# A 64-image convolution, spectral-mixing and FFN kernel: the last 64 expanded channels computed unshifted, and shifted by transfers

## The chip, the cores and the metric

The kernel runs on one core of a Trainium2 chip, in one launch. The metric is device time in microseconds; the number given is the median of several runs. Beside these runs there is one execution under the hardware profiler, and every duration of a single instruction in this document comes from such an execution.

## What is computed

The input is 64 images of 96 channels by 56 x 56 pixels, all in fp32. Each image goes through two layers.

```
# layer 0: inverted residual block with a shift and a channel shuffle
out = silu(bn(einsum('bchw,oc->bohw', x, expand_w)))      # 96 -> 192 channels
out = shift(out)      # quarter 0 one row down, 1 one column right, 2 one row up, 3 one column left
out = channel_shuffle(out, groups=4)
out = silu(bn(bn(depthwise3x3(out)) + bn(out * id_w)))
out = out * sigmoid(grouped(relu(grouped(mean(out)))))    # squeeze and excitation
x   = silu(bn(einsum('bchw,oc->bohw', out, proj_w)) + x)  # 192 -> 96

# layer 1, on the 3136 tokens of an image
t = t + attn(layernorm(t))   # 96 -> 192, relu, FFT over tokens, per-channel complex
                             # scale and relu, inverse FFT, 192 -> 96
t = t + ffn(layernorm(t))    # 96 -> 384 -> 96 with inputs rounded to fp8
```

The shift moves every quarter of the 192 channels by one pixel, with zeros coming in at the edge. It follows the silu of the expansion, so a shifted value is the same number at another place.

## The kernel before, in words

**One image after another, many in flight.** Each image is cut into about sixty kinds of step (x_in, ea_mm, eb_mm, lt, f2_mm and so on), most with several numbered pieces: `ea_mm[3]` is strip 3 of `ea_mm`. The table `PLAN` gives each piece a time relative to its image's start, the image number times `PERIOD` is added, and the pieces of all 64 images are issued in the order of the sum. These times set nothing but an order. Every engine (TensorE = PE, VectorE = DVE, ScalarE = ACT, GpSimd = POOL) and the transfer queue of SyncE (SP) then works strictly in that order, and waits where an operand is not ready. All transfers of the loop are issued by SP. Pieces of up to four images stand between one another: while one image is expanded, the one before is in its convolution, and older ones are in the spectral layer and the FFN.

**Expansion.** The image lies in one buffer `x` (`xi` in the code) with a border of one pixel, on 112 partitions: 96 channels, one partition of ones that brings the bias, and a gap. The 192 expanded channels are kept in two tensors. `e_a` holds the first 32 channels of each of the four quarters, 128 channels, one per partition. `e_b` holds the other 16 channels of each quarter, 64 channels, and to fill the partitions the image is split into two row halves: partitions 0 to 63 hold the upper 28 rows, 64 to 127 the lower 28, each with one row of the other half and the border, which the 3 x 3 convolution needs.

`ea_mm` (L413) computes strips of 8 rows. It shifts by reading: for each quarter a matmul with 32 weight columns reads a window of `x` that is moved by one pixel (`window`), so what lands in PSUM is already shifted. `ea_ev` (L418) applies silu on ACT.

`eb_mm` (L430) does the same for `e_b`. A quarter is 16 channels here, [...] so two quarters with different windows share one block: a table `ex_b` of weights padded with zeros lets the first matmul (e = 0) write one quarter and zeros, and the second (e = 1) add the other. A piece of 7 rows takes eight matmuls: two values of `e`, two row halves `h`, two blocks `u`. There are four such pieces, and a fifth of one row that gives the row which each half needs of the other. `eb_ev` (L443, L445, L446) evicts them with silu into `e_b`.

**Convolution.** The depthwise convolution is divided among engines. For `e_a`, `dw_mm` (L475) does 36 of the 56 rows on PE with diagonal weights; it uses all four buffers of the PSUM pool `psb`. `gt` (L494, L496) does the other 20 rows on DVE in nine taps into `d_vec`. For `e_b`, `lt` (L507, L509) does all rows on DVE in nine taps into `d_last`; `lt[0]` is the middle tap, and it needs all of `e_b`. ACT then applies silu and sums (`dw_ev` L484, `gs` L499, `ls` L512).

**The rest, as far as it is spoken of here.** `se1`, `se2` compute the gate; `pj_mm` (L575 to L586), `pj_add` (L594) and `pj_ev` (L600) project, add `x` and write the tokens `t`. `x_in` (L198) loads the next image into `x` once `pj_add` has read it. `c_mm` (L626), `c_st` (L634), `c_v`, `c_pow`, `sp_v` (L658), `sp_mm`, `sp_ev`, `sp_ld` (L664) and `sp_st` (L683) compute the layernorm's statistics and put them where they are used. `w1_mm` (L696), `w1_ev` (L708), `f1_mm` (L723), `f1_ev` (L735), `f1_st` (L744) do the first matmul and the first part of the FFT and send the spectrum to DRAM; `f2_ld` (L753, L755) fetches it back in another order. The frequency stage is `f2_mm` (L769, L779), `f2_u` (ACT, L794), `f2_s` (DVE, L810, L813), `f2_r` (ACT, L817) and `f2_p` (DVE, L823), in six groups of which `f2_p[5]` is the last in the order. `w2_mm` (L834, L846) reads what `f2_p` wrote, `w2_ev` (L864) evicts, `i1_mm` (L873) and `i1_ev` (L885) begin the inverse, `i1_st` (L892) sends rows to DRAM, `i2_ld` (L897, L898) fetches them in two halves, a one-element `probe` between them waiting for the first half. `i2_mm` (L908) and `i2_ev` (L920) finish the inverse and add to `t`. The FFN is `n_mm` (L608), `n_sq` (L615), `n_v` (L619), `n_pow` (POOL, L936), `n_x` (L942), `x_mm` (L951), `x_ev` (L958), `h_mm` (L964), `h_ev` (L969), `h_b` (L974), `h_q` (L980), `o_mm` (L986), `o_ev` (L991), `o_b` (L996), `o_f` (POOL, L1002), and `o_st` (L1008), which stores the result. Matmul results of the spectral layer go to two large PSUM buffers, `psa`, used in turn; all others to the four of `psb`.

## Time and profile before

| what | value |
|---|---|
| three runs | 6729.68, 6730.21, 6732.37 us; median 6730.21 |
| the profiled execution | 6725.7 us, of which 6723.9 us is the span from the first to the last instruction |
| mean granted TensorE clock | 0.986 |
| busy in the span | PE 6152.3, DVE 5639.2, ACT 4384.5, POOL 1493.4 us |
| DMA | 689.44 MB, mean 103 GB/s |
| DVE waiting for `e_b` at `lt[0]` (L507) | 140.8 us in 64 waits |
| PE in the matmuls that write `ps_eb` (L430) | 367.0 us for 4096 records of 392 columns, 24.9 us for 1024 of 56 |

Two things help in reading. An fp32 matmul of the program is two records in the trace (4 matmuls of 392 columns, 2 values of `e`, 4 pieces, 64 images and two passes are the 4096 of the last row). And a line such as `3062.17 2.84 PE L430 MATMUL ps_eb<-x,ex_b ... x32` reads: from 3062.17 us after the span's start, for 2.84 us, 32 such records, named by what they write and read. In brackets stands how long the engine had been idle before, and what ended that wait.

### The profile page before, as it was taken

What the parts mean: (1) busy time and instruction counts of PE and PEld (TensorE: products, weight loads), DVE (VectorE), ACT (ScalarE), POOL (GpSimd) and SP (SyncE); (2) the same over time, 40 slices, a digit from 0 to 9 for tenths busy, and PEclk for the clock granted to TensorE, in tenths of its full rate; (3) what the DMA queues carried; (4) which work ended last, traced back from release to release, by engine and by line L of the source; (5) the groups of instructions that cost most, each with busy time, mean ns of one, the idle gap of its engine ahead of it and who ended that gap; (6) DMA issues with size and microseconds to landing.
All of it is one profiled execution on the core that took longest, in us unless ns stands there. A gap on an engine that the chain in (4) does not pass through costs nothing.

```text
span 6723.9 us, 246864 instructions
## 1 busy us (share of the span) xinstructions
PE 6152.3 (91%) x107010; PEld 4033.1 (60%) x107010; DVE 5639.2 (84%) x10903; ACT 4384.5 (65%) x8718; POOL 1493.4 (22%) x1035
## 2 busy tenths in 40 slices
PE   6999999999999999999999999999999999999996
PEld 3656655666656666566566666666665656656654
DVE  7888888888888888888888888888888888888884
ACT  2666666666666666666666666666666666666665
POOL 1212212222222222122222222221222222212212
PEclk9999999999999999999999999999999999999997
DMA  3344444344444444443444444444434444444333
GB/s 76 99 104 106 103 104 105 101 102 109 103 103 105 106 104 103 104 109 98 102 109 103 103 104 106 104 103 104 108 100 103 107 103 103 105 103 108 101 96 82
DMA packets 996378, 689.44 MB, mean 103 GB/s; under 512 B 671298, under 2 KB 944522, under 8 KB 995162
## 3 DMA queue, kind: packets, MB, share of 16 engines
q1 hardware_dynamic: 992570, 671.88, 39.1%
q8 instruction: 841, 13.78, 0.9%
q10 hardware_dynamic: 2720, 1.77, 0.1%
q14 instruction: 247, 2.02, 0.1%
HBM read 329.66 MB, written 341.31 MB: 100 GB/s over the span
## 4 chain that ended last, share of the span: by engine, by line
PE 43%; DVE 35%; ACT 12%; DMA 4%; issue 4%; POOL 1%; SPq 1%; POOLq 0%; ACTq 0%; DVEq 0%
PE ps_d L475 10%; DVE ue L813 6%; DVE buf_h L823 5%; DVE s L810 5%; PE psa L873 5%; ACT ue L794 4%; PE ps_ea L413 4%; PE psa L696 4%; PE ps_eb L430 4%; DVE buf_h L708 3%; DVE d_last L509 3%; PE psa L723 3%; DMA buf_h<-rows 3%; PE ps_c L626 3%; DVE y L974 3%
## 5 line engine op out<-in xcount | busy, mean ns | idle before, releaser
L1002 POOL TENSOR_TENSOR o<-t,o 112x448 f32<-112x448 f32 x448 | 688.7, 1537 | 3539.8 <-DVE o L996 1277.9
L509 DVE SCALAR_TENSOR_TENSOR d_last<-e_b,taps,d_last 128x1568 f32<-128x1568 f32 x512 | 1008.6, 1970 | 2.6
L980 ACT CAST h<-y 128x448 fp8e5<-128x448 f16 x1344 | 747.7, 565 | 167.9 <-DVE y L974 167.8
L496 DVE SCALAR_TENSOR_TENSOR d_vec<-e_a,taps,d_vec 128x1120 f32<-128x1120 f32 x512 | 766.1, 1496 | 13.9
L969 ACT CAST y<-ps_h 128x448 f16<-128x448 f32 x1344 | 692.0, 542 | 90.2 <-PE ps_h L964 79.9
L475 PE MATMUL ps_d<-e_a,diag 32*32 32x504 f32 x18432 | 710.6, 590 | 17.0 <-issue 16.9
L936 POOL TENSOR_TENSOR rs<-v,mhalf 112x4 f32<-112x4 f32 x448 | 450.0, 1012 | 1193.0 <-DVE v L620 1193.0
L696 PE MATMUL psa<-w1c,t 112*64 112x96 f32 x14336 | 652.5, 247 | 1.4 <-ACT fs L735 1.4
L696 PEld LDWEIGHTS psa<-w1c,t 112*64 112x64 f32 x14336 | 607.2, 137 | 73.7 <-DVE t L920 35.9
L794 ACT ACTIVATE ue<-psa,fa 128x448 f32<-128x448 f32 (+1 forms) x512 | 358.9, 704 | 381.3 <-DVE ue L813 355.8
L634 DVE BATCH_NORM_STATS2 st<-ps_c 112x6 f32<-112x96 f32 x1792 | 336.3, 249 | 313.4 <-PE ps_c L626 313.4
L475 PEld LDWEIGHTS ps_d<-e_a,diag 32*32 32x32 f32 x18432 | 392.0, 103 | 325.1 <-issue 69.8
L974 DVE TENSOR_SCALAR y<-y,qb 128x448 f16<-128x448 f16 x1344 | 510.2, 384 | 69.1 <-ACT y L969 65.2
L964 PE MATMUL ps_h<-xq,q 96*128 96x448 fp8e5 x1344 | 425.1, 359 | 131.2 <-ACT t L600 109.3
L769 PEld LDWEIGHTS psa<-l_tab,buf_g 128*64 128x64 f32 x7424 | 361.5, 137 | 241.1 <-issue 109.4
L615 ACT ACTIVATE sq<-ps_n 112x384 f32<-112x384 f32 x448 | 220.2, 492 | 430.6 <-PE ps_n L608 430.2
L769 PE MATMUL psa<-l_tab,buf_g 128*64 128x112 f32 x7424 | 414.6, 263 | 83.8 <-DVE ue L813 46.2
L834 PEld LDWEIGHTS psa<-w2a,buf_h 128*64 128x64 f32 (+1 forms) x7424 | 331.8, 135 | 218.8 <-issue 172.2
L653 POOL TENSOR_TENSOR rs<-v,mhalf 112x16 f32<-112x16 f32 (+1 forms) x128 | 338.0, 2640 | 494.0 <-DVE v L648 494.0
L723 PE MATMUL psa<-buf_h,f_tab 56*64 56x384 f32 x3584 | 401.6, 504 | 47.6 <-DVE buf_h L708 46.8
L810 DVE SCALAR_TENSOR_TENSOR s<-psa,fa,ue 128x448 f32<-128x448 f32 (+1 forms) x512 | 325.1, 635 | 137.3 <-ACT ue L794 137.2
L708 DVE SCALAR_TENSOR_TENSOR buf_h<-psa,rs_full 128x768 f32<-128x768 f32 (+1 forms) x512 | 424.8, 850 | 10.2 <-PE psa L696 9.0
(175 smaller groups left out, 12093.1 us busy)
## 6 DMA issues: line engine op xcount, KB each, us to landing
spec<-fs SPq DMA_DIRECT2D x896, 192.0 KB
buf_g<-spec SPq DMA_DIRECT2D x384, 336.0 KB
buf_h<-rows SPq DMA_DIRECT2D x128, 672.0 KB
x<-in_x SPq DMA_DIRECT2D x896, 84.0 KB
out_dram<-o SPq DMA_DIRECT2D x896, 84.0 KB
rows<-buf_g SPq DMA_DIRECT2D x128, 420.0 KB
rows<-buf_g SPq DMA_DIRECT2D x64, 504.0 KB
buf_g<-spec SPq DMA_DIRECT2D x128, 210.0 KB
```

Of the source, the lines that this page charges most:

```text
L475: nc.tensor.matmul(pss[r][j * 32 : j * 32 + 32], lhsT=diag[pr, tap, :], rhs=e_a[pr, r0 : r0 + SR, dx : dx + HW], start=tap == 0, stop=tap ...
L496: nc.vector.scalar_tensor_tensor(d_vec, win, w, d_vec, ALU.mult, ALU.add)
L509: nc.vector.scalar_tensor_tensor(d_last, win, w, d_last, ALU.mult, ALU.add)
L696: nc.tensor.matmul(ps[hc * 64 : hc * 64 + 64, k, 0:C], lhsT=t[:, n0 : n0 + 64], rhs=w1c[:, hc * C : hc * C + C], start=True, stop=True,)
L708: nc.vector.scalar_tensor_tensor(h_v[:, d * NJ + j0 : d * NJ + j0 + n, :], ps[:, 0:n, 0:C], 0.0, rs_full[:, d, j0 : j0 + n].unsqueeze(2).t ...
L769: nc.tensor.matmul(ps[c0 : c0 + 64, k, 0:CP], lhsT=g_v[:, k1, c0 : c0 + 64], rhs=l_tab[:, k1, :], start=True, stop=True,)
L794: nc.scalar.activation(held["ue", b, i][:, q, 0:n, :], held["f2", b, i][:, 0:n, 0:HW], AF.Identity, bias=par[:, 2 + q : 3 + q], scale=par[ ...
L810: nc.vector.scalar_tensor_tensor(held["s", b, i][:, q, 0:n, :], im, par[:, m : m + 1], a, ALU.mult, ALU.add)
L969: nc.scalar.copy(y16, held.pop(("h", b, i)))
L974: nc.vector.tensor_scalar(y16, y16, qb1[:, i % 3 : i % 3 + 1], 0.0, ALU.add, ALU.max)
L980: nc.scalar.copy(held["h8", b, j][:, m, :], held.pop(("y", b, i)), saturate=False)
L1002: nc.gpsimd.tensor_tensor(o32, rows, o16, ALU.add)
```

## The change

`eb_mm` and `eb_ev` no longer shift. The 64 channels are computed at their own place into a new tensor `e_u` of the shape of `e_b`: four pieces of 8, 8, 7 and 7 rows, each with two matmuls of 64 weight columns (one per row half) that read `x` unshifted and use the plain weights `ex_w`. Each half computes the 30 rows that it needs, two of them common to both, so that the fifth piece is gone, and with it `ex_b`. A new step `eb_sh` has four pieces, one per quarter. Each issues two transfers on SP, one per row half, from 16 partitions of `e_u` to the same 16 partitions of `e_b`, moved by a pixel. For the two quarters that move by a row, whole rows of 58 are copied (one run of 1682 or 1624 elements per partition); for the two that move by a column, 29 rows of 55. Border elements that no transfer writes keep the zeros of the start. `e_u` is filled with zeros once, on POOL. The nine taps `lt` read `e_b` as before.

```diff
-    ex_b = const.tile([CP, 2, 2, 2, 16], F32, name="ex_b")
-    nc.vector.memset(ex_b, 0.0)
...
+    e_u = const.tile([128, HH + 2, PAD], F32, name="e_u")
+    nc.gpsimd.memset(e_u, 0.0)
...
-    EB = (((0, HH), 7), ((7, HH + 7), 7), ((14, HH + 14), 7), ((21, HH + 21), 7), ((HH, HH - 1), 1))
+    EB = ((0, 8), (8, 8), (16, 7), (23, 7))
...
-        for e in range(2):
-            for h in range(2):
-                for u in range(2):
-                    p0 = h * 64 + u * 32
-                    nc.tensor.matmul(
-                        ps[p0 : p0 + 32],
-                        lhsT=ex_b[:, e, u].rearrange("p e i -> p (e i)"),
-                        rhs=window(2 * u + e, rows[h], n),
-                        start=e == 0,
-                        stop=e == 1,
-                    )
+        for h in range(2):
+            r1 = 1 + h * (HH - 2) + r0
+            nc.tensor.matmul(
+                ps[h * 64 : h * 64 + 64],
+                lhsT=ex_w[:, 128:MID],
+                rhs=xi[:, r1 : r1 + n, 1 : HW + 1],
+                start=True,
+                stop=True,
+            )
...
+        nc.scalar.activation(e_u[:, r0 : r0 + n, 1 : HW + 1], held.pop(("eb", b, i)), AF.Silu)
+
+    def eb_sh(b, q):
+        dy, dx = SHIFT[q][0] - 1, SHIFT[q][1] - 1
+        for h in range(2):
+            pr = slice(h * 64 + q * 16, h * 64 + q * 16 + 16)
+            y0 = max(h * HH - 1, -dy, 0)
+            y1 = min(h * HH + HH, HW - 1 - dy, HW - 1)
+            to, at = 1 - h * HH, dy - h * (HH - 2)
+            x0, x1 = max(0, -dx), min(HW, HW - dx)
+            if dx == 0:
+                x0, x1 = -1, HW + 1
+            nc.sync.dma_start(
+                out=e_b[pr, y0 + to : y1 + to + 1, x0 + 1 : x1 + 1],
+                in_=e_u[pr, y0 + at : y1 + at + 1, x0 + dx + 1 : x1 + dx + 1],
+            )
```

The table `PLAN` is new in every line, with the row `eb_sh` added; so all steps stand in a new order, on every engine. `PERIOD` is the same. The rows of the steps above, before and after:

```diff
-    "eb_mm": (-24.9502373, -30.5666300, -24.2855462, -28.5828763, -25.9329880),
-    "eb_ev": (-24.4007802, -29.0870142, -23.6123341, -27.8995689, -24.6078971),
+    "eb_mm": (-31.1397290, -24.7310953, -25.9862870, -33.3851630),
+    "eb_ev": (-29.2878297, -22.7025619, -19.4760646, -30.8761649),
+    "eb_sh": (-13.4384953, -6.6214072, -14.8010373, -10.6899699),
...
-    "lt": (
-        -22.5058312, -19.2781395, -16.0020596, -8.0830315, -5.6296105, 10.1142041, 11.3886298, 19.2795806, 21.4543236,
-    ),
...
+    "lt": (-6.4550079, -3.6120828, 7.1928163, 9.3198177, 9.7271989, 13.9581033, 19.5751277, 20.9508824, 24.2387198),
...
-    "f2_p": (147.3373312, 156.4376915, 150.8056372, 162.7962275, 161.2485624, 169.6535678),
...
+    "f2_p": (146.9434761, 150.0630941, 147.2744764, 160.9872322, 154.5577496, 162.5258346),
```

So `lt[0]` stands at -6.5 instead of -22.5, just behind the last piece of `eb_sh`, and the last group of `f2_p` at 162.5 instead of 169.7. On SP one image's order in this place is: `i2_ld[1]` of the image before, `eb_sh[2]`, `eb_sh[0]`, an `o_st`, `eb_sh[3]`, an `o_st`, `eb_sh[1]`, `sp_st[1]`, `sp_ld[1]`, `f1_st[0]`.

## The prediction

> **What bounds the kernel now.** I read the page first (busy shares, then the chain), then the busy time of three successive images, then one image cut at its turning points, then single engines in order of time.
>
> ```profile
> span 6723.9 us, 246864 instructions
> PE 6152.3 (91%) x107010; PEld 4033.1 (60%) x107010; DVE 5639.2 (84%) x10903; ACT 4384.5 (65%) x8718; POOL 1493.4 (22%) x1035
> PE 43%; DVE 35%; ACT 12%; DMA 4%; issue 4%; POOL 1%; SPq 1%; POOLq 0%; ACTq 0%; DVEq 0%
> ```
>
> TensorE is busiest, but VectorE is close behind, and the chain changes between them: no single engine bounds the kernel.
>
> ```profile
> 3016.00:3119.10 103.10, 94.59 (x1668) 62.09 (x1664) 87.56 (x170) 68.37 (x136) 23.07 (x17) 1.00 0.40 103
> 3119.10:3222.20 103.10, 95.73 (x1694) 62.71 (x1680) 87.74 (x169) 68.37 (x136) 22.47 (x17) 1.00 0.42 105
> ```
>
> After length come PE, PEld, DVE, ACT, POOL, clock, DMA share. An image takes 103.1 us; PE works 95.3 of it (7.8 idle), DVE 88. 63 such laps are 6495 us; 229 us of the span are filling and emptying. Cut at i2_mm, dw_mm, f2_mm and w2_mm[3]:
>
> ```profile
> 3072.00:3108.40 36.40, 35.24 (x707) 25.08 (x707) 34.65 (x56) 22.33 (x46) 11.12 (x10) 1.00 0.37 97
> 3108.40:3119.30 10.90, 10.90 (x287) 6.21 (x288) 10.26 (x11) 4.46 (x8) 2.20 (x1) 1.00 0.54 131
> 3119.30:3160.10 40.80, 34.90 (x525) 23.59 (x516) 33.31 (x62) 30.66 (x59) 3.40 (x2) 1.00 0.35 86
> 3160.10:3175.00 14.90, 14.58 (x165) 7.45 (x163) 8.45 (x45) 9.78 (x24) 6.48 (x3) 1.00 0.57 150
> ```
>
> Stages 1 and 2 fill both engines. Stage 3 (the frequency stage) is a DVE and ACT chain with PE idle 5.9 us. Stage 4 is the round trip of the rows through DRAM; eb_mm (L430) is its filler:
>
> ```profile
> 3062.17 2.84 PE L430 MATMUL ps_eb<-x,ex_b 112*32 112x392 f32 x32
> 3064.82 0.94 PE L413 MATMUL ps_ea<-x,ex_w 112*32 112x448 f32 x8
> 3065.58 3.01 PE L430 MATMUL ps_eb<-x,ex_b 112*32 112x56 f32 x48
> 3068.52 0.77 PE L986 MATMUL ps_o<-h,q 128*112 128x448 fp8e5 x3
> ...
> 3072.01 2.52 PE L908 MATMUL psa<-r_tab,buf_h 64*48 64x56 f32 x112 [1.47 <-DMA buf_h<-rows]
> ```
>
> PE fills this round trip and still waits 1.47 us for the rows. So eb_mm taken out of here gains nothing unless other PE work is moved in. On DVE two waits lie nearby:
>
> ```profile
> 3054.59 0.76 DVE L634 BATCH_NORM_STATS2 st<-ps_c 112x6 f32<-112x96 f32 x4 [3.16 <-PE ps_c L626]
> 3055.26 0.79 DVE L823 SCALAR_TENSOR_TENSOR buf_h<-ue,s 128x280 f32<-128x280 f32 x2
> ...
> 3069.19 1.06 DVE L507 TENSOR_SCALAR d_last<-e_b,taps 128x1568 f32<-128x1568 f32 x1 [2.12 <-ACT e_b L443]
> ```
>
> f2_p[5] (L823), which releases w2_mm[3] and with it stage 4, stands behind a c_st that waits 3.16 us.
>
> [...] four ps_ea of 32 columns share 0.76 us per strip, (2.46 - 0.94) / 2 from groups of 24 and 8 records. [...]
>
> **The change part by part.**
>
> *PE, removed and added.* Each fp32 matmul shows as two records (passes). Before, an image has 4 x 392 + 56 = 1624 columns, twice (two zero-padded weights) in two passes: 6496. From 3062.17 to 3068.52 less one ea_mm (0.76) is 5.6 us, 0.86 ns a column; ea_mm gives 0.76 / 896 = 0.85. After: 2 x 448 + 2 x 392 = 1680 columns once, in two passes, two halves of 64 side by side: 3360 x 0.85 = 2.9 us. If the 64-wide tiles run as f1_mm does (L723, 384 columns: 1.65 - 0.88 = 0.77 us for 8 records, four side by side, 1.0 ns a column), 3.4; if the two didn't overlap, 5.7. I take 2.9: 2.7 us saved per image, 170 us in all. Lower bound nothing, upper 2.7.
>
> *Where PE work moves.* With one image folded into a lap, the changed order puts ea_mm[1] and [2] from stage 1 into stage 4 (2 x 0.76 = 1.5 us less in stage 1), and c_mm[0] to [2] (1.36 for their 12 records) with i1_mm[1] (1.65) from ahead of w2_mm[3] to behind it. Between w2_mm[3] and i2_mm PE then has 14.6 - 2.7 + 1.5 + 1.4 + 1.65 = 16.4 us. The round trip proper runs from i1_mm[2]'s end (3061.28) to i2_mm (3072.0): 10.7 us for eviction, rows written, rows read. Its filler was 9.25 us (to 3070.53) and is now four c_mm 1.8, eb_mm 2.9, three ea_mm 2.3, five h_mm 1.0, two o_mm 1.2, sp_mm 0.2 = 9.4: the wait of 1.4 us stays, and eb_mm's 2.7 us are gained in stages 1 and 3, where ea_mm, c_mm and i1_mm leave. From w2_mm[3] to i2_mm: 1.65 + 1.65 + 0.2 (h_mm) + 1.4 + 1.5 (i1_mm[2]) + 10.7 = 17.1 us instead of 14.95.
>
> *DVE.* The same 115 steps with the same work, moved. lt[0] and lt[1] (1.0 + 1.8) leave stage 4 for behind i2_ev, some h_b go the other way, more lt fall ahead of the first f2_s: from the first i2_ev to there 50.4 us of work instead of 47.9. In stage 3 pj_add[4] to [7] (1.5), two o_b, h_b and c_st[0] go behind f2_p[5]: 25.7 us instead of 28.4, without the 3.16.
>
> *ACT.* Four evictions (two of 448 columns at 0.55, as L418; two at 0.50) instead of 4 x 0.50 + 2 x 0.21: 2.1 for 2.4. ACT is busy 68 of 103; nothing.
>
> *SP and DMA.* Eight issues per image. Issues of this kind take 0.39 (buf_h<-rows) to 0.47 (x<-in_x, median): 3.8 us. They stand between i2_ld[1] and sp_st[1], sp_ld[1], f1_st[0], interleaved with two o_st. In before sp_st[1] went out 3.9 us after i2_ld[1], f1_st[0] 10.3 us after. Now some 6 to 7 us lie ahead, and four sp_ld take 3.3 more; but before f1_ev[0] PE has two f1_mm, two w1_mm, three n_mm, i2_mm and more to do (over 10 us), and before w1_mm[5], the first that needs the sp transfers, some 17. I cost this at zero; without that cover it is 3 us a lap. Bytes: 0.83 MB on 10.6 (103 GB/s x 103.1 us); four of the eight are 464 runs of 220 B. DMA share 0.42 leaves room.
>
> *The new wait.* lt[0] (L507's successor) waits for the last shift instead of for ACT. Count from i2_mm's start T: i2_ld[1] goes out at T + 0.65 (3072.65), twelve issues follow, eight transfers may be under way at once, so the seventh or eighth waits until i2_ld[1] has landed (4.8 us): last issue T + 7.5. x<-in_x, 384 runs of 224 B, has the packets of its first issue done within 2.2 us (issued 3036.58), so landing at about T + 10; from T + 8.5 (all at once) to T + 13 (double transfer time, one by one). DVE gets to lt[0] at T + 1.5 + eight i2_ev (0.56), three n_v (0.67), two w1_ev (0.9), three n_x (0.5) = 11.3, with 0.9 of waits 12.2. Cost zero, with 2 us in hand; at the late bound 1 us a lap. Behind lt[0] on DVE stand w1_ev and n_x, which release PE.
>
> *Once.* One POOL memset of e_u (1.5 us, as e_b), long before the first eviction at 42 us; ex_b's three DVE instructions go. Zero.
>
> **The sum.** Two limits. By PE: 103.1 - 2.7 = 100.4 if its 7.8 us of idle stays. By the DVE and round-trip ring: T to i2_ev 1.5; 50.4 + 2.2 of gaps (50.15 measured on 47.9 of work); 25.7 + 3.9 of gaps (35.5 measured, less 28.4 and 3.2); then about 1 to w2_mm[3] and 17.1 to the next i2_mm: 101.9. PE has 3 us less to do inside stage 3 and 1.5 less in stage 1, so some of those gaps close; I take 101.25, between the two. 1.85 x 63 = 117 us off 6725.7 (the profiled execution; its span 6723.9) gives 6609. The runs' median 6730.2 lies 4.5 above that execution; I give 6612.
>
> **The rivals.** *All of it is passed on* and the gaps close too: lap 99.6 to 100.4, 6725.7 - 63 x (2.7 to 3.5) = 6505 to 6556. For: c_st no longer blocks f2_p[5], and PE has slack in stage 3. Against: 50.4 us of DVE work with hardly a gap.
> *Nothing arrives*: DVE's ring gets 103 us, because lt[0] and lt[1] lost their idle place in stage 4 and the gaps of stage 3 (ACT's ue ping-pong) stay or grow. 6717 to 6743.
> *Slower*: the shifts land late at lt[0]. DVE is gapless there, so each us late is a us per lap. Up to T + 12 it is free; past T + 14 the gain is used up; at T + 16 the lap is 105, 6725.7 + 63 x 1.9 = 6845. It needs the 220 B runs to take several times what 224 B runs took, or o_st[2], ahead of the last pair on SP, to wait for POOL. For: SP is in order, and four transfers of 464 runs follow i2_ld[1] on the same engines. Against: x<-in_x.
> *Not as said*: the 64-wide halves don't overlap; then 5.7 us as before and only the order counts, within 1% either way; small, inside the cases above.
>
> **Chances.** Forecast (6556 to 6700) 0.55; all passed on 0.25; nothing 0.07; slower 0.13. Faster 0.80, same 0.07, slower 0.13; 0.2% (13 us) is about what this kernel's measurement can tell from no change. Range 6510 to 6728: it leaves out the slower case and the tails.
>
> **What would show it.** Right: ps_eb near 3 us an image with 64-column tiles; i2_mm still waiting about 1.4 us for the rows; no wait for e_b at lt[0]; c_st waits behind f2_p[5]; lap near 101.3. Wrong: lt[0] waiting on DMA e_b<-e_u; PE idle over 10 us a lap; DVE idle in stage 3 above 5 us; eb_mm near 5.7 us.

## The result: 4.3% slower

The changed kernel takes 7021.7 us (median of 4 runs, 7013.7 to 7024.7) against 6729.9 of the kernel before on the same chip: 1.043 times as long, with an interval of 1.041 to 1.045. The prediction said 6612, in a range of 6510 to 6728. The profiled execution after is 7021.5 us, its span 7019.8 us, the mean granted TensorE clock 0.951 instead of 0.986.

The first lines of the profile after, and its chain (the work that ended last, followed back from the end, by engine):

```profile
span 7019.8 us, 239130 instructions
PE 6234.1 (89%) x102914; PEld 4101.1 (58%) x102914; DVE 5671.2 (81%) x10900; ACT 4365.1 (62%) x8590; POOL 1494.9 (21%) x1036
DVE 29%; PE 23%; DMA 18%; ACT 10%; issue 10%; POOL 5%; SPq 5%; DVEq 0%; POOLq 0%; ACTq 0%
```

PE issues 4096 records fewer, and yet is busy 82 us more: the same matmuls last longer. In the chain PE and DVE have given 26 points, most of them to DMA (4% before, 18% now), to SP's queue and to "issue". Now one image cut at i2_mm, dw_mm, f2_mm and the last w2_mm group, then two successive laps (columns as before: us, PE, PEld, DVE, ACT, POOL, clock, DMA share, GB/s):

```profile
3091.50:3132.90 41.40, 37.68 (x691) 25.73 (x690) 34.71 (x52) 21.54 (x45) 9.61 (x9) 0.92 0.46 109
3132.90:3143.30 10.40, 10.35 (x292) 6.48 (x288) 10.40 (x12) 4.50 (x9) 0.00 (x0) 1.00 0.50 124
3143.30:3183.20 39.90, 35.76 (x500) 25.75 (x500) 32.67 (x59) 28.17 (x53) 6.68 (x3) 0.87 0.35 84
3183.20:3200.40 17.20, 16.69 (x140) 8.33 (x132) 9.99 (x49) 13.79 (x32) 7.99 (x4) 1.00 0.54 136
2984.20:3091.50 107.30, 95.91 (x1496) 62.82 (x1496) 86.30 (x168) 67.47 (x133) 22.50 (x16) 0.94 0.44 106
3091.50:3198.80 107.30, 99.16 (x1603) 66.07 (x1606) 87.36 (x167) 67.02 (x134) 23.23 (x16) 0.92 0.44 107
```

A lap is 107.3 us instead of 102.7 to 103.1. The clock, 1.00 in all four stages of the image shown before, is 0.92 in stage 1 and 0.87 in stage 3. Three places show what happens. First, the end of stage 4 on PE:

```profile
3081.53 0.88 PE L422 MATMUL ps_eb<-x,ex_w 112*64 112x392 f32 x4
3082.64 0.97 PE L422 MATMUL ps_eb<-x,ex_w 112*64 112x448 f32 x4
3088.23 1.63 PE L422 MATMUL ps_eb<-x,ex_w 112*64 112x392 f32 x8
3091.34 0.26 PE L671 MATMUL ps_dev<-eye,dev 112*12 112x112 f32 x1 [0.29 <-DVE dev L658]
3091.52 2.52 PE L908 MATMUL psa<-r_tab,buf_h 64*48 64x56 f32 x112
```

The new eb_mm takes 3.5 us an image, and i2_mm no longer waits for the rows. Second, DVE (line, last group of f2_p, c_st, and the first tap lt[0]) and SP (the queue from i2_ld[1] on):

```profile
3072.09 0.81 DVE L823 SCALAR_TENSOR_TENSOR buf_h<-ue,s 128x280 f32<-128x280 f32 x2 [0.19 <-ACT s L817]
3078.46 2.18 DVE L634 BATCH_NORM_STATS2 st<-ps_c 112x6 f32<-112x96 f32 x12 [3.40 <-PE ps_c L626]
3105.86 1.04 DVE L507 TENSOR_SCALAR d_last<-e_b,taps 128x1568 f32<-128x1568 f32 x1 [1.48 <-DMA e_b<-e_u]
```

```profile
3091.30 0.38 SPq L898 DMA_DIRECT2D buf_h<-rows  x1
3092.04 2.47 SPq L445 DMA_DIRECT2D e_b<-e_u  x4
3094.55 1.52 SPq L1008 DMA_DIRECT2D out_dram<-o  x2
3096.12 2.71 SPq L445 DMA_DIRECT2D e_b<-e_u  x2
3098.92 1.78 SPq L1008 DMA_DIRECT2D out_dram<-o  x2
3100.75 1.26 SPq L445 DMA_DIRECT2D e_b<-e_u  x2
```

c_st waits behind f2_p now, as forecast. But from i2_mm's start T = 3091.5 the last issue of a shift begins at T + 9.9, not T + 7.5, and ends at T + 10.5, and lt[0] begins at T + 14.3, after a wait that names the shift. (Over 48 laps in the middle the last issue ends at T + 10.8, and lt[0] begins at T + 14.2.) The second group of `eb_sh` takes 2.7 us for two issues because the latter of them waits until i2_ld[1], the `buf_h<-rows` ahead of the first, has landed; over the whole run SP waits for that (us in total, times, longest):

```profile
SPq L445 <- DMA buf_h<-rows: 60.8, 53, 3.6
```

Third, f2_mm in stage 3, twice the same group of 32 records:

```profile
3035.49 3.25 PE L769 MATMUL psa<-l_tab,buf_g 128*64 128x112 f32 x32 [3.23 <-DMA buf_g<-spec]
3049.57 1.75 PE L769 MATMUL psa<-l_tab,buf_g 128*64 128x112 f32 x32 [0.29 <-ACT o L991]
```

After a wait of 3.2 us for the spectrum from DRAM, the group takes 3.25 us; 14 us later it takes 1.75. The clock's records grant 0.50 for the first and 1.00 for the second.

**The table that the rest rests on.** For each run 48 laps in the middle were cut on the trace's records at three points: first i2_mm to first f2_s (A), from there to the end of the last f2_p (B), from there to the next i2_mm (C). "Idle" is PE's idle time per lap, "half" the time per lap in which the records grant it half clock. Half of that is counted as lost, an estimate from the group above (3.25 us at half clock, 1.75 at full); "work" is then what remains of the lap, lap - idle - half / 2 (some of the half clock falls into idle time, so that it is good to 1 or 2 us). Each ratio is against before on the same chip.

| kernel | us | to before (interval) | lap | A | B | C | idle | half |
|---|---|---|---|---|---|---|---|---|
| before | 6730 | 1 | 102.7 | 52.3 | 35.6 | 14.9 | 7.1 | 1.6 |
| after | 7022 | 1.043 (1.041 to 1.045) | 107.3 | 57.3 | 31.4 | 18.6 | 10.4 | 9.0 |
| order_only | 6936 | 1.032 (1.031 to 1.034) | 106.1 | 53.9 | 31.1 | 21.1 | 8.4 | 5.9 |
| edit_only | 7321 | 1.089 (1.088 to 1.091) | 112.0 | 61.0 | 35.6 | 15.4 | 14.6 | 13.3 |
| no_shifts | 6786 | 1.010 (1.008 to 1.011) | 103.9 | 54.0 | 31.3 | 18.6 | 8.5 | 5.9 |
| unread_shifts | 6842 | 1.017 (1.015 to 1.018) | 104.6 | 54.6 | 31.4 | 18.6 | 9.2 | 6.0 |
| edit_no_shifts | 6770 | 1.006 (1.005 to 1.008) | 103.5 | 53.1 | 35.6 | 14.8 | 9.3 | 3.6 |
| tap_thrice | 7006 | 1.042 (1.040 to 1.043) | 107.1 | 58.0 | 30.5 | 18.6 | 9.0 | 6.2 |
| sh_split | 6837 | 1.016 (1.015 to 1.018) | 104.6 | 54.6 | 31.3 | 18.7 | 9.0 | 6.8 |
| split_ea | 6797 | 1.010 (1.008 to 1.012) | 103.7 | 54.9 | 30.1 | 18.7 | 8.9 | 3.1 |

Read by its last columns, the change is this: work fell by 2.4 us (94.8 to 92.4), idle rose by 3.3, and half clock by 7.4 us, worth 3.7. Together +4.6 us a lap, 290 us in 63 laps.

### The profile page after: what moved, and what is told of

It is laid out like the page before. It is cut to its first block, busy times and chain, and to the rows that moved or that the text cites. A ratio compares the mean times of both kernels' runs of the same rounds, so it can differ in the third digit from the quotient of the medians.

```text
span 7019.8 us, 239130 instructions
## 1 busy us (share of the span) xinstructions
PE 6234.1 (89%) x102914; PEld 4101.1 (58%) x102914; DVE 5671.2 (81%) x10900; ACT 4365.1 (62%) x8590; POOL 1494.9 (21%) x1036
## 4 chain that ended last, share of the span: by engine, by line
DVE 29%; PE 23%; DMA 18%; ACT 10%; issue 10%; POOL 5%; SPq 5%; DVEq 0%; POOLq 0%; ACTq 0%
DMA buf_g<-spec 9%; DVE s L810 5%; DVE ue L813 5%; POOL rs L653 3%; PE psa L696 3%; PE psa L769 3%; DMA e_b<-e_u 3%; ACT ue L794 3%; DMA spec<-fs 3%; DVE d_last L509 3%; DMA buf_h<-rows 3%; PE psa L723 3%; DVE buf_h L708 3%; DVE buf_h L823 3%; DVE ps_pj L594 2%
## 5 line engine op out<-in xcount | busy, mean ns | idle before, releaser
L509 DVE SCALAR_TENSOR_TENSOR d_last<-e_b,taps,d_last 128x1568 f32<-128x1568 f32 x512 | 943.7, 1843 | 0.3
L696 PE MATMUL psa<-w1c,t 112*64 112x96 f32 x14336 | 753.3, 259 | 109.2 <-DVE buf_h L708 90.2
L696 PEld LDWEIGHTS psa<-w1c,t 112*64 112x64 f32 x14336 | 669.9, 145 | 193.0 <-DVE buf_h L708 106.5
L496 DVE SCALAR_TENSOR_TENSOR d_vec<-e_a,taps,d_vec 128x1120 f32<-128x1120 f32 x512 | 735.6, 1437 | 2.6
L769 PE MATMUL psa<-l_tab,buf_g 128*64 128x112 f32 x7424 | 497.0, 295 | 212.3 <-DMA buf_g<-spec 194.0
L475 PE MATMUL ps_d<-e_a,diag 32*32 32x504 f32 x18432 | 661.0, 590 | 0.0
L769 PEld LDWEIGHTS psa<-l_tab,buf_g 128*64 128x64 f32 x7424 | 442.5, 159 | 339.5 <-issue 260.3
L974 DVE TENSOR_SCALAR y<-y,qb 128x448 f16<-128x448 f16 x1344 | 461.6, 349 | 202.5 <-ACT y L969 193.0
L735 ACT COPY fs<-psa 128x768 f32<-128x768 f32 x448 | 357.1, 809 | 310.9 <-PE psa L723 307.2
L964 PE MATMUL ps_h<-xq,q 96*128 96x448 fp8e5 x1344 | 448.4, 366 | 72.6 <-ACT t L600 49.6
L723 PE MATMUL psa<-buf_h,f_tab 56*64 56x384 f32 x3584 | 416.9, 541 | 57.5 <-DVE buf_h L708 54.5
```

The costliest lines, as they stand in the source:

```text
L475: nc.tensor.matmul(pss[r][j * 32 : j * 32 + 32], lhsT=diag[pr, tap, :], rhs=e_a[pr, r0 : r0 + SR, dx : dx + HW], start=tap == 0, stop=tap ...
L496: nc.vector.scalar_tensor_tensor(d_vec, win, w, d_vec, ALU.mult, ALU.add)
L509: nc.vector.scalar_tensor_tensor(d_last, win, w, d_last, ALU.mult, ALU.add)
L696: nc.tensor.matmul(ps[hc * 64 : hc * 64 + 64, k, 0:C], lhsT=t[:, n0 : n0 + 64], rhs=w1c[:, hc * C : hc * C + C], start=True, stop=True,)
L723: nc.tensor.matmul(ps[d * 64 : d * 64 + 64, hc, 0 : 4 * C], lhsT=f_tab[hc * 64 : hc * 64 + HW, :], rhs=h_v[hc * 64 : hc * 64 + HW, n0 : n0 ...
L769: nc.tensor.matmul(ps[c0 : c0 + 64, k, 0:CP], lhsT=g_v[:, k1, c0 : c0 + 64], rhs=l_tab[:, k1, :], start=True, stop=True,)
```

## The experiments

Ratios outside the table have intervals of 0.0015 to 0.0023 either way. The first expectations speak of two theories: the "clock theory" blames the new order, which leaves PE idle in two places of an image, after which it runs at half clock; the "shift theory" blames the transfers.

**Order, edit, transfers taken apart.** order_only is the code of before under the new table, with a place for the fifth piece of eb_mm and eb_ev; edit_only is the new code under the old table, all eight transfers together between the last eb_ev and lt[0]; no_shifts is the changed kernel without eb_sh. Their edits, in this order, cut to the rows of the table and the changed lines (the code of `eb_mm`, `eb_ev` and `eb_sh` is that of the diff above):

```diff
-    "eb_mm": (-31.1397290, -24.7310953, -25.9862870, -33.3851630),
-    "eb_ev": (-29.2878297, -22.7025619, -19.4760646, -30.8761649),
-    "eb_sh": (-13.4384953, -6.6214072, -14.8010373, -10.6899699),
+    "eb_mm": (-31.1397290, -24.7310953, -25.9862870, -33.3851630, -24.6000000),
+    "eb_ev": (-29.2878297, -22.7025619, -19.4760646, -30.8761649, -19.4000000),
...
```

```diff
+    "eb_mm": (-24.9502373, -30.5666300, -24.2855462, -28.5828763),
+    "eb_ev": (-24.4007802, -29.0870142, -23.6123341, -27.8995689),
+    "eb_sh": (-23.6000000, -23.5000000, -23.5500000, -23.4500000),
...
```

```diff
-    "eb_sh": (-13.4384953, -6.6214072, -14.8010373, -10.6899699),
...
-        win = e_b[:, dy : dy + HH, dx : dx + HW]
+        win = e_u[:, dy : dy + HH, dx : dx + HW]
...
-        x_in, ea_mm, ea_ev, eb_mm, eb_ev, eb_sh, dw_mm, dw_ev, gt, gs, lt, ls, se1_mm, ...
+        x_in, ea_mm, ea_ev, eb_mm, eb_ev, dw_mm, dw_ev, gt, gs, lt, ls, se1_mm, ...
```

> The order of the changed kernel with the old way of expanding (padded weights, five pieces, no e_u, no transfers); the fifth piece stands beside the others. Clock theory (the new order leaves TensorE idle in two places per image, and there its clock is granted at half): as slow as the changed kernel, 6950 to 7080 us, with the clock well under 0.97 and ps_eb at 5.6 us an image. Shift theory (the eight transfers are the cost: e_b late at lt[0], the queue and the DMA engines loaded): near the kernel before, 6650 to 6780 us.

> The changed expansion and its eight transfers in the order of the kernel before; the transfers stand directly behind the last eb_ev, ahead of sp_ld[0] and i2_ld[1]. Clock theory: 6700 to 6850 us; f2_mm finds its data, but eb_mm's 2.7 us are gone as filler of the rows' round trip, so i2_mm waits some 4 us for the rows and the clock may drop there. Shift theory: 6900 us or more, lt[0] waiting for e_b<-e_u by 3 us or more per image.

> The changed kernel without eb_sh: lt reads e_u directly, so the shift of the last 64 channels is left out; everything else and the order stay. Clock theory: still over 6900 us, clock under 0.97, TensorE still waiting for buf_g<-spec at the first f2_mm. Shift theory: 6600 to 6720 us, clock back at 0.98.

Measured 6936, 7321 and 6786. So neither theory has it all: from before to the new order +3.4 us a lap, from the old to the new expansion within that order -2.2, from no transfers to eight +3.4. The order's part is all idle and half clock (1.3 us, and 4.3 at half rate). In edit_only lt[0] waits about 10 us a lap, 10.9 in the one shown. The profile names another transfer, which lt[0] does not read; the wait is for e_b, for without the transfers, in edit_no_shifts below, all waits at lt[0] come to 4.9 us, and here to 642.3. DVE stands, and PE behind it:

```profile
3354.32 3.77 PE L910 MATMUL psa<-r_tab,buf_h 64*48 64x56 f32 x112 [3.63 <-DMA buf_h<-rows]
3361.94 0.35 PE L673 MATMUL ps_dev<-eye,dev 112*12 112x112 f32 x1 [3.85 <-DVE dev L660]
```

```profile
3360.43 1.04 DVE L509 TENSOR_SCALAR d_last<-e_b,taps 128x1568 f32<-128x1568 f32 x1 [10.86 <-DMA rs_full<-rs]
```

So with the old order, and all eight transfers behind the last eb_ev, the kernel is slower still. Whether the old order would do with the transfers split and only the taps moved was not run.

**Is it the wait at lt[0], or the load of the transfers?** unread_shifts is after with all transfers, but the taps read e_u (the one-line edit above), so that nobody waits for a shift.

> The changed kernel with all eight transfers per image, but the taps lt read e_u, the unshifted tensor: nobody waits for a transfer. It leaves out the shift of the last 64 channels in the convolution. Without the transfers at all the lap was 103.9 us (6786), with them and the wait 107.3 (7022). Wait theory (lt[0] stands at the head of a gapless VectorE, and what it loses PE loses, clock included): 6780 to 6830, since only the wait is gone. Load theory (eight issues on SP and packets on the DMA engines hold up i2_ld, f1_st and f2_ld): 6950 to 7020. Halfway would be both.

6842. The load costs 0.7 us a lap (103.9 to 104.6), the wait 2.7 (104.6 to 107.3). In the lap shown (T = 3032.9) lt[0] ran at T + 12.0, where the prediction had put DVE's arrival (T + 12.2); over 48 laps it was T + 12.8:

```profile
3044.89 1.03 DVE L507 TENSOR_SCALAR d_last<-e_u,taps 128x1568 f32<-128x1568 f32 x1
```

**Later taps.** If DVE has no gap there, lt[0] and lt[1] could be put behind the landing at no cost.

```diff
-    "lt": (-6.4550079, -3.6120828, 7.1928163, ...
+    "lt": (7.0000000, 7.1000000, 7.1928163, ...
```

lt_mid has -0.3 and 4.5 for these two.

> The changed kernel with lt[0] and lt[1] moved in the order from -6.5 and -3.6 to 7.0 and 7.1, directly ahead of lt[2]; the transfers and everything else stay. Wait theory: the shifts have landed by then, VectorE has other work meanwhile, and the time is that of the run in which nobody waited for a transfer: 6820 to 6860 (6842 there). Load theory: the later place changes little, 6980 to 7030.

> The changed kernel with lt[0] and lt[1] at -0.3 and 4.5 instead of -6.5 and -3.6: later than the shifts' landing, but apart from one another and from lt[2]. Wait theory: 6830 to 6900, since the wait is gone and PE's releases are not blocked by 5.6 us of taps in one piece, as in the run that had them in one block (7134). If the taps are in the way anywhere behind the first n_x, because PE then waits for w1_ev and falls to half clock: 7000 to 7130.

7134 and 7108 (1.060 and 1.056): both worse than after, against the wait theory as stated. lt_mid's DVE and PE, with T = 3033.2, show why:

```profile
3048.14 0.55 DVE L619 TENSOR_REDUCE v<-sq 112x4 f32<-112x384 f32 x1 [1.99 <-ACT sq L615]
3049.54 0.96 DVE L708 SCALAR_TENSOR_TENSOR buf_h<-psa,rs_full 128x768 f32<-128x768 f32 x1 [0.64 <-PE psa L696]
...
3051.27 1.04 DVE L507 TENSOR_SCALAR d_last<-e_b,taps 128x1568 f32<-128x1568 f32 x1
```

```profile
3051.95 1.49 PE L696 MATMUL psa<-w1c,t 112*64 112x96 f32 x32
3058.40 2.83 PE L696 MATMUL psa<-w1c,t 112*64 112x96 f32 x32 [2.85 <-DVE buf_h L708]
```

DVE does have a hole, at T + 13 to T + 16, where it waits for ACT and PE; lt[0] and lt[1] fill it. Put later, they leave it empty and stand in front of the w1_ev that release PE, which waits 2.85 us and then takes 2.83 us for the next group instead of 1.49, nearly twice as long, as the group of f2_mm did at half clock. DVE is gapless because the taps lie where they lie. At the two later places tried, late taps are no way out; the shifts have to be early.

**Earlier shifts.** sh_act issues all eight on ACT's queue behind evictions that come some us earlier in the order; sh_split only those of the two quarters that move by a row, and the other four on SP directly behind i2_ld[1]:

```diff
-    "eb_mm": (-31.1397290, -24.7310953, -25.9862870, -33.3851630),
-    "eb_ev": (-29.2878297, -22.7025619, -19.4760646, -30.8761649),
-    "eb_sh": (-13.4384953, -6.6214072, -14.8010373, -10.6899699),
+    "eb_mm": (-31.1397290, -28.9000000, -29.0000000, -33.3851630),
+    "eb_ev": (-29.2878297, -27.2000000, -27.3000000, -30.8761649),
+    "eb_sh": (-24.5000000, -14.7000000, -26.1000000, -14.8000000),
...
-            nc.sync.dma_start(
+            (nc.sync if q % 2 else nc.scalar).dma_start(
```

> The changed kernel, the whole computation, with the eight transfers issued on ACT's queue instead of SP's, right behind the evictions (-25.5 to -20), and for that eb_mm[2], [1] and their evictions 3 to 7 us earlier in the order; lt[0] and lt[1] stay at -6.5 and -3.6. Without the transfers this order of eb_mm gave 6793. Wait theory: the shifts land before lt[0], nothing waits, 6790 to 6850. Price theory: the transfers cost by being issued and moved, wherever; ACT loses 4 to 5 us per image between the evictions and the first n_sq, and i2_ld shares the engines with them: 6900 to 7020.

> The changed kernel, the whole computation, with the transfers of two quarters on ACT's queue, right behind the evictions in the stage of the rows' round trip (-26.1 and -24.5), and those of the other two on SP directly behind i2_ld[1] (-14.8 and -14.7), the evictions some us earlier; lt stays. Wait theory: the last shift lands at about T + 8 to 10, ahead of VectorE's T + 12, ACT issues only four (2.4 us) where it is not the bound: 6820 to 6870, as in the run with the transfers unread (6842). Price theory: four issues still hold up n_sq, or four in a row on SP hold up sp_st and o_st: 6900 to 7000.

sh_act: 7049 (1.047), above both forecasts and no better than after, though lt[0] no longer waits (17.1 us in all, in the first image). In the lap shown ACT stood 3.5 us ahead of n_sq: 2.2 us because the last pair of issues waited until an earlier shift had landed, 1.3 for the pair itself. DVE stood behind it:

```profile
3127.70 1.27 ACTq L445 DMA_DIRECT2D e_b<-e_u  x2
3129.02 0.49 ACT L615 ACTIVATE sq<-ps_n 112x384 f32<-112x384 f32 x1 [3.52 <-PE ps_n L608]
```

sh_split: 6837, the whole computation in the time of the run in which no shift was read. Over 48 laps its last issue ends at T + 6.2 and lt[0] runs at T + 12.6, unhindered. The lines for lt[0] in all 64 images (busy us, mean ns of one, idle ahead of it), after and then sh_split, have 103.1 us of waits and one single wait, that of the first image:

```profile
L507 DVE TENSOR_SCALAR d_last<-e_b,taps 128x1568 f32<-128x1568 f32 x64 | 66.2, 1035 | 103.1 <-DMA e_b<-e_u 76.5 <-issue 13.6 <-DMA rs_full<-rs 8.8
L507 DVE TENSOR_SCALAR d_last<-e_b,taps 128x1568 f32<-128x1568 f32 x64 | 65.9, 1029 | 15.3 <-DMA e_b<-e_u 15.3
```

That settles the shifts: 2.7 of their 3.4 us are the wait, and it is their lateness, since half of the issues moved elsewhere take it away. The remaining 0.7 stays with the transfers.

**The order: the trip of the spectrum and the clock.** The last part of the spectrum leaves f1_mm[6] (L723), goes to DRAM and back, and f2_mm needs it. In before, three strips of ea_mm ([3], [4] and [6], 2.3 us) and dw_mm cover this trip; in after dw_mm follows f1_mm[6] directly, and PE then waits at f2_mm (the line at 3035.49 above). PE behind f1_mm[6], before and after:

```profile
3105.18 0.93 PE L723 MATMUL psa<-buf_h,f_tab 56*64 56x384 f32 x8
3106.04 2.46 PE L413 MATMUL ps_ea<-x,ex_w 112*32 112x448 f32 x24
```

```profile
3021.15 0.88 PE L723 MATMUL psa<-buf_h,f_tab 56*64 56x384 f32 x8
3021.96 10.31 PE L475 MATMUL ps_d<-e_a,diag 32*32 32x504 f32 x288
```

The waits of f2_mm for the spectrum rise from 18.1 to 194.0 us. Four runs try this: ea_back puts two strips back (with their evictions), with the transfers, without them (no_shifts_ea_back), and with the split ones (split_ea); tap_thrice adds useless work instead:

```diff
-    "ea_mm": (15.1071188, -27.4826408, -26.8524884, 11.9911650, 8.0334218, -23.9701817, 21.0193630),
+    "ea_mm": (24.3000000, -27.4826408, -26.8524884, 11.9911650, 8.0334218, -23.9701817, 24.5000000),
...
```

```diff
-        for tap in range(third * 3, third * 3 + 3):
+        for n, tap in enumerate((0, 0, 0, 1, 2) if third == 0 else range(third * 3, third * 3 + 3)):
...
+            again = third == 0 and n < 2
...
-                        stop=tap == 8,
+                        stop=tap == 8 or again,
```

> The changed kernel with two strips of ea_mm (0 and 6) moved from ahead of f1_mm[6] to behind it, directly ahead of dw_mm, so that TensorE has 1.5 us more to do while the last part of the spectrum goes to DRAM and back. Clock theory: the wait at the first f2_mm and the half clock behind it mostly go: 1.5 to 3 us a lap, 6830 to 6930 us. Shift theory: no change beyond 0.3%, 7000 to 7040 us.

> The changed kernel without the eight transfers, the taps reading e_u, and with ea_mm[0] and ea_mm[6] put back between f1_mm[6] and dw_mm, as in the kernel before. It leaves out the shift of the last 64 channels. Cover theory (those strips covered the trip of the spectrum through DRAM, without them PE stops at f2_mm and goes on at half clock): the step costs as much here as with the transfers, 6939 against 7022, so 6690 to 6720, and the half clock behind f2_mm halves. Shift theory (the order costs nothing by itself, and only lets the late shifts through): 6770 to 6800, as without the edit.

> The changed kernel with its first tap of dw_mm computed three times instead of once, the first two as closed groups that the third overwrites: 2.4 us more of PE work per image, useless, between f1_mm[6] and f2_mm, where the three ea_mm strips stood before. Clock theory (it is the pause ahead of f2_mm and the half clock after it that cost): the pause and the half clock in the frequency stage shrink, and the time falls in spite of the work, 6900 to 6990. Work theory (PE is the bound, idle costs nothing more than itself): 7020 to 7170.

> sh_split with ea_mm[0] and [6] back between f1_mm[6] and dw_mm. Wait theory: 27 to 80 us below it, 6760 to 6830; still not below the kernel before, since even without any transfer this order gave 6759. Price theory: 6850 to 6960.

ea_back 6939 (1.033), no_shifts_ea_back 6759 (1.004), split_ea 6797 (1.010), each against the run without the strips: they are worth 1.0, 0.55 and 0.66% by the ratios (68, 37 and 44 us). Without the transfers the run missed its 6690 to 6720: f2_mm's waits for the spectrum fell from 191.6 to 70.7 us there, but stage 1 grew by 1.1 us. Of that 0.8 is f1_mm[6], now ahead of the strips: it takes 1.7 us instead of 0.9, since three of its four matmuls wait for w1_ev on DVE. So a part of PE's pause had moved there. tap_thrice is the cleaner test. Its 7006.3 us lie between the two forecasts (6900 to 6990, 7020 to 7170): the 2.4 us more of PE work a lap did not make the kernel faster than after (7021.7; the intervals of the ratios overlap), and not slower either, because the pause was filled and the half clock in stage 3 fell from 5.1 to 2.4 us a lap. The group of f2_mm in before, in after and in tap_thrice (busy us, mean ns of one, idle ahead of it):

```profile
L769 PE MATMUL psa<-l_tab,buf_g 128*64 128x112 f32 x7424 | 414.6, 263 | 83.8 <-DVE ue L813 46.2 <-DMA buf_g<-spec 18.1 <-ACT y L969 17.3
```

```profile
L769 PE MATMUL psa<-l_tab,buf_g 128*64 128x112 f32 x7424 | 497.0, 295 | 212.3 <-DMA buf_g<-spec 194.0 <-ACT o L991 9.2 <-DVE ue L813 6.7
```

```profile
L770 PE MATMUL psa<-l_tab,buf_g 128*64 128x112 f32 x7424 | 443.5, 274 | 107.3 <-DMA buf_g<-spec 63.1 <-DVE ue L814 34.2 <-ACT o L992 9.5
```

**Is the saved matmul work worth anything where it was?** edit_no_shifts is edit_only without transfers, the taps reading e_u.

> The order of before with the new expansion (2.6 us less PE work ahead of i2_mm) and no transfers, the taps reading e_u: it leaves out the shift of the last 64 channels. The prediction's reading: that work only filled the trip of the rows through DRAM, so the wait at i2_mm grows by it and the time stays, 6690 to 6740, with perhaps some half clock behind the longer pause. If PE is the bound through that stage too: lap 2 us shorter, 6590 to 6640.

6770, 1.006 (1.0047 to 1.0077), outside both forecasts: 2.4 us of work less a lap, and slower. The waits at i2_mm for the rows, before and in edit_no_shifts (us in total, times, longest), went from 33.5 us to 169.0:

```profile
PE psa L908 <- DMA buf_h<-rows: 33.5, 35, 3.9
```

```profile
PE psa L909 <- DMA buf_h<-rows: 169.0, 64, 4.2
```

That is 2.1 us a lap, nearly all that was saved, and 1.9 us of half clock a lap follow the waits in stage 1, where before has none in the 48 laps. In before the useless half of the old eb_mm filled this wait.

**Attempts to do better, that failed.** lt_early (no transfers) moved the two taps ahead of i2_mm; x2 has two buffers for the image, so that x_in comes one image sooner, and eb_mm in the frequency stage with the transfers behind it (e_u lies in the buffer `d` there, and POOL clears its border for every image); late_back and sh_act_ea add the two strips to lt_late and sh_act. The edits of lt_early, then those of x2 (cut to the table and the buffer):

```diff
+    "eb_mm": (-31.1397290, -28.9000000, -29.0000000, -33.3851630),
+    "eb_ev": (-29.2878297, -26.1000000, -26.2000000, -30.8761649),
...
+    "lt": (-22.1000000, -21.9000000, 7.1928163, ...
```

```diff
+    "eb_mm": (-54.2000000, -52.7000000, -52.8000000, -56.8000000),
+    "eb_ev": (-53.0000000, -50.9000000, -51.2000000, -55.5000000),
+    "eb_sh": (-45.9000000, -45.7000000, -46.0000000, -45.8000000),
+    "lt": (-25.0000000, -22.0000000, 7.1928163, ...
...
+    x_buf = [const.tile([CP, PAD, PAD], F32, name=f"x_{i}") for i in range(2)]
...
+                out=x_buf[b % 2][p0 : p0 + 48, 1 + i * RPC : 1 + (i + 1) * RPC, 1 : HW + 1],
```

> The changed kernel without the eight transfers, the taps reading e_u (it leaves out the shift of the last 64 channels), with lt[0] and lt[1] put where the kernel before has them, into VectorE's idle time ahead of i2_mm (-22.1 and -21.9), and for that eb_mm[2], [1] and their evictions some 3 to 7 us earlier in the order, still in the same stage. Ring theory (from i2_mm to the first f2_s VectorE is the bound, and the two taps that the transfers push into that stretch cost their own 2.8 us there): lap 101.2 to 102, so 6620 to 6670, against 6786. Cover theory (that stretch is bounded by PE's pauses, its half clock and the trip of the spectrum): 6750 to 6800.

> The whole computation, with the transfers. The image has two buffers x, used in turn, and x_in loads one image further ahead, so that eb_mm need not wait for pj_add: eb_mm stands at the end of the frequency stage (-57 to -52), the transfers at -46, lt[0] and lt[1] at -25 and -22, in VectorE's idle time ahead of i2_mm. e_u lies in d_buf, which is free there, and POOL clears its border columns once per image. Ring theory: VectorE has 2.8 us less between i2_mm and the first f2_s, the wait for the shifts is gone, PE has 3 us less ahead of i2_mm and some of it idle in the frequency stage: lap 101.3 to 102.5, 6640 to 6710, below the kernel before. Rivals: eb_mm in the frequency stage delays f2_mm and VectorE's chain there by all of its 3 us, or POOL's clearing, queued behind o_f, holds the transfers: 6740 to 6850.

> lt_late with ea_mm[0] and [6] also put back between f1_mm[6] and dw_mm. If the wait for the shifts and the uncovered trip of the spectrum are separate costs: 6842 less 27 (without the transfers the strips gave 27 us), so 6800 to 6830. If the strips' larger gain of 82 us with the waiting lt[0] came from the trip itself: 6750 to 6790.

> sh_act with ea_mm[0] and [6] back between f1_mm[6] and dw_mm. If the transfers cost nothing once they are early, this is the run without transfers and with the strips back, 6759, give or take 30: still not below the kernel before, because what is left is the order's. If they have a price of their own: 6850 to 6950.

lt_early 6793 (1.009), the same as no_shifts: A stayed at 54.0 us, so the ring theory's 2.8 us of taps do not set it. x2 7211 (1.072), far above both its forecasts: A was 54.2 us, no less than without transfers, and B grew by 6.4 to 37.8. A part of the reason is visible on PE, where each piece of eb_mm waits for an eviction on ACT; the rest was not followed up:

```profile
3279.71 0.73 PE L990 MATMUL ps_o<-h,q 128*112 128x448 fp8e5 x3 [0.96 <-ACT d L438]
3281.30 0.97 PE L425 MATMUL ps_eb<-x,ex_w 112*64 112x448 f32 x4 [0.86 <-ACT o L995]
3282.92 1.63 PE L425 MATMUL ps_eb<-x,ex_w 112*64 112x392 f32 x8 [0.65 <-ACT d L438]
```

late_back 7060 (1.049), sh_act_ea 7018 (1.043): each below the run without the strips (1.060, 1.047), and both above all their forecasts.

**Why are the transfers late?** wide_runs is edit_only with the eight transfers cut across 128 partitions instead of along 16, so that they carry as much but do not shift. It asks whether the few partitions make the runs slow:

```diff
-            pr = slice(h * 64 + q * 16, h * 64 + q * 16 + 16)
...
+            if q % 2:
+                rows = slice(1 + (q - 1 + h) * 4, 5 + (q - 1 + h) * 4)
+                nc.sync.dma_start(out=e_b[:, rows, 2 : HW + 1], in_=e_u[:, rows, 1:HW])
+            else:
+                rows = slice(17 + (q + h) * 3, 20 + (q + h) * 3)
+                nc.sync.dma_start(out=e_b[:, rows, :], in_=e_u[:, rows, :])
```

> The order of before with the new expansion and the eight transfers together (7321 before, lt[0] waiting 10.9 us for them), but each transfer is cut across 128 partitions instead of along 16: four of 128 x 4 rows of 220 bytes, four of 128 runs of 696 bytes, nearly the same bytes and as many 220-byte runs. They do not shift: it leaves out the shift of the last 64 channels. Narrow theory[...]: the wait at lt[0] falls to 4 to 6 us, time 6850 to 7050. Run theory (runs of 220 bytes between two tiles are slow whatever the partitions, or the eight issues set the time): the wait stays at 9 to 11 us, 7250 to 7350.

7176 (1.066); the waits at lt[0] fell from 642.3 to 516.7 us in all, 10.0 to 8.1 a lap: between the two forecasts. The packets do get faster (median of those of 220 bytes 16 ns instead of 31), but eight issues and a landing are most of it, with 128 partitions as with 16 (in edit_only the eight issues of one image took 5.7 us from 3349.32 on):

```profile
3058.14 2.48 SPq L444 DMA_DIRECT2D e_b<-e_u  x4
3060.66 2.71 SPq L441 DMA_DIRECT2D e_b<-e_u  x4
```

```profile
3066.83 1.04 DVE L503 TENSOR_SCALAR d_last<-e_b,taps 128x1568 f32<-128x1568 f32 x1 [8.44 <-DMA rs_full<-rs]
```

5.2 us of issuing and 3.5 us more until the last has landed.

No version here beats the kernel before. The best with the whole computation is split_ea at 1.010, and even without any transfer this order gives 1.004.

## Why the prediction was wrong

Its model of the lap was a ring of 54.1 us (A), 29.6 (B) and 18.1 (C), from which it then took 101.25. Measured: 57.3, 31.4 and 18.6. The step that failed worst is the new wait, which it cost at zero. Step by step:

- *PE, removed: 2.7 us.* Nearly right. The matmuls that write ps_eb were busy 380.1 us before and 226.4 after, 2.4 us an image less (5.9 to 3.5). That two halves of 64 columns (112*64 in the trace of after, 112*32 in that of before) would run side by side was the author's estimate; 3.5 us an image, where it put 5.7 without overlap, bears it out.
- *Stage 4: 17.1 us, i2_mm still waiting 1.4.* Nearly right in length (C is 0.5 us longer), wrong in kind: the profile has i2_mm waiting for the rows in 1 of 64 cases. PE, not the trip, now sets the stage, so each us put there counts in full: with the old eb_mm in this place, in order_only, C is 2.5 us longer still.
- *Stage 3: 25.7 us of DVE work, gaps 3.9.* The work is right (31.4 less 5.8 idle is 25.6); the gaps are 5.8, not 3.9. The prediction counted ea_mm[1] and [2], which change their stage, and did not look at [3], [4] and [6], which stay in stage 1 but no longer stand behind f1_mm[6], where they covered the trip of the spectrum; this cover it put at nothing. B is 1.8 us longer than forecast; tap_thrice shows 0.9 of it to be pause and half clock at f2_mm.
- *The new wait: last issue at T + 7.5, landing at T + 10, cost zero with 2 us in hand.* This is the step that failed worst: A is 3.2 us longer than forecast, the largest single miss. DVE's arrival was right (T + 12.3 without the transfers, over 48 laps), and so was A without them (54.0). Wrong was the time of SP. An issue of a shift took 0.6 us, not 0.39 to 0.47; in the image shown the eight took 4.8 us instead of 3.8, and the four o_st between them 3.2. That a pair is held back until i2_ld[1] has landed was foreseen (SP's 4941 issues of after carry eight semaphores in turn, and each waits for the transfer that used its own before; before's 4429 do the same), but i2_ld[1] took 6.6 us to land (mean of 48 laps) and not 4.8; in the image shown its packets of 384 bytes took 22 ns each up to 3095.5, and from there to 3097.5, beside those of the first shifts, 54 to 72 (medians of half a us). So the last issue began at T + 9.8 on average, and the data were there at T + 13.9: of the 3.9 us missed, 2.3 lie ahead of the last issue, and 1.6 between its start and its landing. The price of an issue could have been read off before: on the same queue a transfer of `spec<-fs` takes 0.62 us to issue there and one of `rs_full<-rs` 0.76 (medians), and the prediction took two of the cheaper kinds as its measure. Between no_shifts and after A grows by 3.3 us; 2.7 of this are the wait and 0.6 the load. The wait costs more than it shows: DVE's line for lt[0] has 103.1 us, 16.3 of them in the first image, so 1.4 us a lap; the rest goes with half clock in stage 1 (3.9 us a lap, 0.7 when unread), which PE gets while DVE's releases are late (its waits for w1_ev at f1_mm are 54.5 us, and 14.0 when unread).
- *The choice of 101.25 instead of 101.9*, on the ground that "some of those gaps close", cost the last 0.65: they grew.
- *"100.4 if its 7.8 us of idle stays".* The sum takes PE's idle as staying or shrinking, and its speed as given. Neither held: idle rose by 3.3 us and half clock by 7.4. That is also why the gain of 2.4 us in work never showed by itself.
- *Two readings of before.* The cut at 3160.10 is the end of f2_p; w2_mm[3] begins at 3161.16, so the 14.95 us set against the 17.1 begin 1 us earlier than these. And from the first i2_ev to the first f2_s the image shown has 51.1 us, not 50.15; over 48 laps A is 52.3 us in before. The forecast of A held all the same, as no_shifts shows. (6609 and 4.5 are 6613.5, not 6612; nothing hangs on it.)

The slower rival had the place right ("the shifts land late at lt[0]"), and its threshold (free up to T + 12). Neither of the causes that it asked for came: the runs of 220 bytes took 18 ns (median) against 16 for those of 224 bytes, and o_st waits for POOL in 10 of its 896 issues. It was the issuing, and then the time to land. Its price of one us per us late was too low: lt[0] begins 1.4 us later than in unread_shifts, and A is 2.7 us longer. It missed the order's part. It got a chance of only 0.13 because the packets of x<-in_x were taken as the yardstick, and packets were the lesser part of what was late.

The order's 3.4 us are settled as idle and half clock. Which single move of the table brings each of them is only partly settled: the strips account for 37 to 68 us, depending on what else is late. What keeps no_shifts_ea_back 0.4% above before, apart from the 0.8 us at f1_mm[6], is open.

## What to carry to other kernels

When a step leaves a place in the order, ask what it covered there, and not only what it cost: PE work that "only fills" a round trip can also hold the clock. Taking it away brought here 1.9 us of half clock a lap and 0.6% more time, even without any transfer (edit_no_shifts). A copy by the queue cost here its issue on the engine that issues it (0.6 us), the waiting of everything behind it, and from the end of the issue to the landing 3.1 us on average (4.0 in edit_only, where all eight go together); count the last one of a series from the moment its queue is free, and split a series between two queues where neither has to go late. An engine that looks gapless can be so only because one step fills a hole: moving that step later opens the hole (lt_late and lt_mid, 1.060 and 1.056 against 1.043).

## What the hardware showed

- The clock fell to half after several short waits, not only after one longer one. Its records in before and after know only 1.0 and 0.5, and all but the last of each run last a multiple of 3.41 us. In the 3.41 us ahead of a drop PE was idle 2.0 us in all (median over some 100 drops in after; 1.8 in before, there in one gap), and in after the longest single gap was 1.2 us (median). In the windows of after that no drop followed PE was idle 2.0 us at most, and over 1.8 in six of some 1660.
- Runs of 220 bytes between two tiles on the same 16 partitions took 18 ns (median) in after, and 31 in edit_only, where all eight transfers went together; spread over 128 partitions, in the same place of the same order, they took 16 (wide_runs). In sh_act, on the 16 partitions but over 9 us, they took 16 too, so that in these four runs 16 partitions were much slower than 128 only where the eight transfers went together. Runs of 224 bytes from DRAM (`x<-in_x`) took 16 ns in before and after, as the wide ones of 220 between two tiles did.
- An issue of such a transfer took 0.5 to 0.65 us of the issuing queue where nothing held it up, SP in after or ACT in sh_act; SP's four in sh_split took 0.9 to 1.2 (medians), for a reason that the runs don't show. In the lap of sh_act shown above the last pair of issues ended at 3128.97 us, and n_sq, behind it on ACT, began at 3129.02.
